# New instruction lengths and waiting rules in the planner that orders a macaron layer's instructions

## The chip, the cores and the metric

The kernel runs on one core of one Trainium2 chip. The metric is the device time of one execution in microseconds (us), taken as the median of several executions. The core has five instruction queues that matter here. PE is TensorE, the matrix engine; DVE is VectorE; ACT is ScalarE; POOL is GpSimd; SP is SyncE, which issues every DMA of this kernel. Each of them works through its own list of instructions strictly in order, and they wait for each other by semaphores.

## The reference, cut to what matters

The input x is 4 x 2048 x 256. The layer is a "macaron": half a feed-forward block, attention, and half a feed-forward block again, each on a normalised x.

```python
x = x + 0.5 * ffn(layernorm(x), w_gate, w_up, w_down)
x = x + attn(layernorm(x), Wq, Wk, Wv)        # causal, one head of 256
x = x + 0.5 * ffn(layernorm(x), w_gate, w_up, w_down)

def ffn(x, w_gate, w_up, w_down):             # hidden width 704
    h = silu(fp4_linear(x, w_gate)) * fp4_linear(x, w_up)
    return fp4_linear(h, w_down)

def fp4_linear(x, w):                         # both sides rounded to FP4 in blocks of 16
    return einsum('bsk,nk->bsn', fp4(x), fp4(w))
```

`fp4` takes the largest absolute value of each block of 16, divides by it over 6, rounds to the nearest of eight magnitudes and multiplies the scale back. It is done to the inputs of all three linear maps, so x and h pass through DVE several times before each product.

## The kernel before, in words

The 2048 rows of each of the 4 batches are cut into 8 pairs of 128-row tiles, so there are 32 pairs in all. One pair goes through: load, first layernorm (`ln_first`), FP4 of x (`x1`), gate and up products (`gu1`), FP4 of h (`hh1`), down product (`down1`), second layernorm (`lnattn`), the transposed copy of x for attention (`xattn`), the value and the key-side products (`vy`), scores, softmax (`exps`), weights times values (`pv`), third layernorm (`lnlast`), and the second feed-forward block (`x2`, `gu2`, `hh2`, `down2`). `step(n)` writes these stages for different pairs beside each other: pair n is in its scores while pair n+4 is in its gate and up products and n-2 in its second block. The last pair is cut into its two tiles, which go one behind the other.

Names that the text uses, with who writes them:

- `xn` normalised x (ACT), `xt` the running x in float32. A layernorm is: row sums, squares with row sums (ACT), a chain of seven small operations on POOL that ends in the mean times the inverse deviation (`fnm`, `anm` or `gnm` by stage), and the scaling back on ACT.
- `xs`, `xinv`, `xsh`, `xsl` block scales of x, `xf` its FP4 value; `xqT` the transposed halves of x that PE reads (a DMA transpose issued by SP).
- `pg`, `pu` PSUM results of gate and up, one buffer of two banks each; `h` is Silu of `pg` (ACT) times `pu` (DVE). Until Silu has read `pg`, the next gate product can't start.
- `hs`, `hinv`, `hsh`, `hsl`, `hf`: the same steps for h; `hT` its transposed halves. `po` (two buffers) takes the down product and is added to `xt` by DVE.
- `y` (`y16`) the key-side product, `vv` the values, `xT` transposed x, `ps` scores (two buffers), `sc` scores in SBUF, `pp` and `pT` softmax weights and their transposes.
- `gu`, `gwork`, `dwork`, `dw`, `wguT`, `wdT`, `tops`, `mx`, `cwp`: the preparation of the weights, FP4 as well, which runs once at the start beside the first pairs.

The order of the instructions isn't the order of the Python. Every operation is recorded (`Record`, `Op`) with what it reads and writes, and then `Record.order` plans: `_cost` gives each operation two lengths, `busy` (how long its engine is taken) and `late` (when its result can be seen), and each pair of dependent operations gets a lag. `_pass` then plays the program: at each point it takes the engine that can start first, and on it the waiting operation with the best rank, where being not ready yet costs `patience` and a change of the activation table costs `SWITCH`. A pass backwards gives new ranks, and six rounds of this for each of the fifteen entries in `POLICIES` are compared by `_lost`, PE's idle time in the first 500 us and after it in the planner's own clock. The best entry for each half is taken, and the list that results is what `emit` issues, one queue per engine (line 362, which is why every instruction of the profile is put down to that line). The planner's clock has no influence at run time: it only sets the order in each queue. What is computed, by which engine and in which buffers, is fixed.

In `_pass` three resources have rules of their own. DMA transposes are served one after the other (`served`). POOL shares its way to SBUF with some DVE operations (`op.locks`: two wide inputs, or a `tensor_scalar` on 16-bit data, none from PSUM): before the change a POOL operation is put off to the end of the DVE operation running (`locked`), and while one is put off (`kept`), DVE operations that lock are ranked lower by `PORT`. A change of activation table delays the operation by 1290.

Of the kernel before, what the change touches and what calls it, by code (L numbers as in the profile page):

```python
# [17 lines left out]
AF = mybir.ActivationFunctionType  # L18
ALU = mybir.AluOpType
# [33 lines left out]
LN2 = 0.6931471805599453  # L53
BYTES = {F32: 4, I32: 4, F16: 2, BF16: 2, U16: 2}
SWITCH = 17600.0
PORT = 500.0
ROUNDS = 6
POLICIES = [(soon, 60.0, lead) for lead in (0.0, 10000.0, 20000.0) for soon in (50.0, 100.0, 150.0, 200.0, 300.0)]
MIDDLE = 500000.0
# [1 line left out]
LATENCY = 1900.0  # L61
# [93 lines left out]
class Record:  # L155
# [53 lines left out]
    def _cost(self, op):  # L209

        size = lambda v: v.at.size
        views = op.outs + op.ins
        n = max(map(size, views[:1] + (op.ins[:1] if op.method == "tensor_reduce" else [])))
        psum = any(v.tile.pool.psum for v in views)
        accum = isinstance(op.kwargs.get("accum_out"), View)
        if op.engine == "PE":
            t = max(n, 64) / 2.4 + 2.2
            if op.ins[0].dtype == F32:
                t *= 2 if op.method == "transpose" or "is_transpose" in op.kwargs else 4
            return t, t + 65  # L220
        if op.engine == "SP":
            if op.method == "dma_start_transpose":
                return 1240, 2250 + max(0, n - 500) * 1.2
            op.load = n * 4 * P / RATE if op.outs else 0
            return 490, LATENCY + op.load + 500 * (not op.outs)
        if op.engine == "POOL":
            t = 110 if op.method == "memset" else 850 if ALU.pow in op.args else 350
            return t, t
        if op.engine == "ACT":
            t = 95 + n * (0.75 if psum else 0.833) + 90 * accum  # L230
            t += 90 * sum(isinstance(op.kwargs.get(k), View) for k in ("scale", "bias"))
            return t, t + 105 * (not accum)
        many = sum(size(v) > 1 for v in op.ins)
        op.locks = not psum and (many > 1 or op.method == "tensor_scalar" and BYTES[op.ins[0].dtype] == 2)
        fast = not psum and all(BYTES[v.dtype] == 2 for v in views)
        if op.method == "reciprocal":
            t = 60 + 6.25 * n
        else:
            t = 65 + n * (1.042 if not fast else 0.26 if op.method == "tensor_scalar" else 0.52) + 65 * accum
        return t, t + 95  # L240

    def order(self):

        for pool in self.pools:
            for ring in pool.rings.values():
                for k, t in enumerate(ring):
                    if k >= t.n:
                        t.first.deps.update(dict.fromkeys(ring[k - t.n].ops, True))  # L250
                    if k:
                        t.first.deps.setdefault(ring[k - 1].first, False)
                    t.first.deps.pop(t.first, None)
        for op in self.ops:
            for u in op.after:
                op.deps.setdefault(u, False)
            op.users = {}
        for op in self.ops:
            for u, data in op.deps.items():
                u.users[op] = u.late + 24 if data else u.busy  # L260

        best = [None, None]
        for policy in POLICIES:
            lead = {op: op.lead * policy[2] for op in self.ops}
            rank = {op: 88.0 * op.index - lead[op] for op in self.ops}
            for _ in range(ROUNDS):
                start, out, end = self._pass(rank, False, policy, policy)
                for h, value in enumerate(self._lost(start, end)):
                    if best[h] is None or value < best[h][0]:
                        best[h] = (value, policy, start, rank)  # L270

                back, _, _ = self._pass({op: -start[op] - op.busy for op in self.ops}, True, policy, policy)
                rank = {op: -back[op] - op.busy - lead[op] for op in self.ops}
        (_, one, start, rank1), (_, two, _, rank2) = best

        part = {op: min(1.0, max(0.0, (start[op] - MIDDLE) / 50000.0 + 0.5)) for op in self.ops}
        rank = {op: rank1[op] * (1.0 - part[op]) + rank2[op] * part[op] for op in self.ops}
        return self._pass(rank, False, one, two)[1]
# [7 lines left out]
    def _pass(self, rank, back, one, two):  # L286


        free = dict.fromkeys(("PE", "ACT", "DVE", "POOL", "SP"), 0.0)
        waiting, held = {e: [] for e in free}, ("PE", "POOL")  # L290
        ready, start = dict.fromkeys(self.ops, 0.0), {}
        if back:
            nxt, left = {op: [] for op in self.ops}, {op: len(op.users) for op in self.ops}
            for op in self.ops:
                for v, lag in op.users.items():
                    nxt[v].append((op, v.busy + lag - op.busy))
        else:
            nxt, left = {op: list(op.users.items()) for op in self.ops}, {op: len(op.deps) for op in self.ops}
        for op in self.ops:
            if not left[op]:  # L300
                waiting[op.engine].append(op)
        kept = False
        table, out, end, landed, served, locked, clock = None, [], 0.0, 0.0, 0.0, 0.0, Counter()
        while len(out) < len(self.ops):
            best = None
            if not any(waiting.values()):
                raise RuntimeError("the order goes in a circle")
            for e, ops in waiting.items():
                if ops:
                    t = max(free[e], min(ready[op] for op in ops))  # L310
                    if best is None or t < best[0]:
                        best = (t, e)
            t, e = best
            soon, patience = (one if t < MIDDLE else two)[:2]
            now = [op for op in waiting[e] if ready[op] <= t + soon]
            op = min(now, key=lambda o: (
                rank[o] + patience * max(0.0, ready[o] - t) + SWITCH * (o.table is not None and o.table != table)
                + PORT * (kept and e == "DVE" and o.locks)
            ))
            t = max(t, ready[op])  # L320
            if e == "POOL" and not back and op.method != "memset":

                kept = t < locked
                if kept:
                    free[e] = locked + 1.0
                    continue
            if op.table is not None and op.table != table:
                table, t = op.table, t + 1290
            waiting[e].remove(op)
            out.append(op)  # L330
            start[op], more = t, 0.0
            if back:
                pass
            elif e == "PE":

                k = int(t // WINDOW)
                more = op.busy if k and clock[k - 1] < IDLE * WINDOW else 0.0
                clock[k] += op.busy + more
            elif op.load:
                landed = max(landed, t + LATENCY) + op.load  # L340
                more = landed - t - op.late
            elif e == "SP" and op.outs:
                served = max(served + 1.7 * op.outs[0].at.size + 100, t + op.late)
                more = served - t - op.late
            elif e == "DVE" and op.locks:
                locked = t + op.busy
            elif e == "POOL" and op.method != "memset":
                more = (775.0 if ALU.pow in op.args else 275.0) - op.busy
            free[e] = t + op.busy + (more if e in held else 0.0)
            end = max(end, t + op.late + more)  # L350
            for u, lag in nxt[op]:

                ready[u] = max(ready[u], t + lag + (more if e in held or u.deps.get(op) else 0.0))
                left[u] -= 1
                if not left[u]:
                    waiting[u.engine].append(u)
        return start, out, end
# [787 lines left out]
```

## Time and profile before

| | |
|---|---|
| runs of the kernel | median 1195.94 us of 3 (1193.82 to 1197.42) |
| the profiled execution | 1194.8 us, span from first to last instruction 1193.1 us |
| busy in the span | PE 1156.1, DVE 1064.1, ACT 845.4, POOL 254.9 us |
| matmuls | 8665 |
| activation table loads | 84, 107.8 us in all |
| TensorE clock granted | 0.999 of full over the span |
| DMA transposes on SP's queue | 152 `pT`, 128 `hT`, 65 `xqT`, 64 `xT`, 2 `wguT` |

PE is the engine to look at: it is busy for 97% of the span. A matmul is pipelined; the length that the profile gives it (274 ns for 256 columns) runs until its last result, while the next one starts after 110 ns. So PE's idle time in a stretch, not its instructions' lengths, tells what is lost there. In the same way DVE's and ACT's operations overlap their neighbours by some 0.08 us when they don't wait for each other.

### The profile page before, as it was taken

How to read it: one execution, taken by the hardware profiler on the slowest of the kernel's cores; microseconds unless marked ns; L12 is line 12 of the kernel's file. 1: busy time of each engine (PE TensorE's matmuls, PEld its weight loads, DVE VectorE, ACT ScalarE, POOL GpSimd, SP SyncE). 2: the span in 40 equal slices, each digit the busy share in tenths (PEclk: the TensorE clock that was granted, in tenths of full speed). 3: DMA queues.
4: the chain of work that ended last, by engine and by line, in shares of the span. 5: the costliest groups of instructions: out<-in, count | busy, mean ns of one | idle time of the engine just before them, and what ended most of it. 6: DMA issues, size and time to landing. Idle time of an engine off the chain costs nothing.

```text
span 1193.1 us, 23867 instructions
## 1 busy us (share of the span) xinstructions
PE 1156.1 (97%) x8665; PEld 843.8 (71%) x8665; DVE 1064.1 (89%) x2677; ACT 845.4 (71%) x1694; POOL 254.9 (21%) x706
## 2 busy tenths in 40 slices
PE   3999999999999999999999999999999999999997
PEld 1676677777687777777777777777777777777775
DVE  8998999998879999998888999999887999978776
ACT  8788886676568777775776986776758776766552
POOL 4122331121032222212222230222212222010020
PEclk9999999999999999999999999999999999999999
DMA  7353646763665565655755465666556454665553
GB/s 236 55 100 71 109 88 110 140 129 71 107 131 103 105 116 120 113 93 111 134 102 81 95 114 104 131 131 120 92 104 113 88 93 87 114 117 96 102 111 85
DMA packets 452710, 128.92 MB, mean 108 GB/s; under 512 B 434672, under 2 KB 451824, under 8 KB 452592
## 3 DMA queue, kind: packets, MB, share of 16 engines
q1 hardware_dynamic: 452592, 127.39, 57.0%
q8 instruction: 68, 1.11, 0.4%
q14 instruction: 50, 0.41, 0.1%
HBM read 11.34 MB, written 8.39 MB: 17 GB/s over the span
## 4 chain that ended last, share of the span: by engine, by line
PE 68%; DVE 15%; ACT 12%; issue 2%; DMA 2%; POOL 1%; SPq 0%; DVEq 0%; ACTq 0%
PE po L362 30%; PE pg L362 14%; PE pu L362 14%; PE ps L362 10%; DVE h L362 5%; ACT xn L362 3%; ACT L362 2%; DVE hs L362 2%; ACT hf L362 2%; ACT h L362 1%; DVE xt L362 1%; DMA hT<-h 1%; ACT pp L362 1%; DVE xs L362 1%; DVE sc L362 1%
## 5 line engine op out<-in xcount | busy, mean ns | idle before, releaser
L362 PEld LDWEIGHTS <-xqT 128*128 128x128 f16 x3072 | 299.7, 98 | 161.1 <-issue 6.2
L362 PE MATMUL po<-wdT,hT 128*128 128x256 f16 x2176 | 262.6, 274 | 5.9 <-DMA hT<-h 5.6
L362 PE MATMUL pg<-wguT,xqT 128*128 128x384 f16 (+1 forms) x1536 | 258.9, 312 | 4.3 <-ACT h L362 2.3
L362 PE MATMUL pu<-wguT,xqT 128*128 128x384 f16 (+1 forms) x1536 | 253.3, 312 | 0.1
L362 PEld LDWEIGHTS <-hT 128*128 128x128 f16 x2176 | 213.2, 98 | 39.8 <-DMA hT<-h 7.6
L362 PE MATMUL ps<-xT,y 128*128 128x512 f16 (+2 forms) x960 | 200.9, 347 | 1.0 <-DVE mc L362 1.0
L362 PE MATMUL po<-vv,pT 128*128 128x257 f16 (+1 forms) x1632 | 194.4, 272 | 0.4
L362 PEld LDWEIGHTS <-pT 128*128 128x128 f16 x1632 | 157.9, 97 | 33.3 <-issue 2.3
L362 ACT ACTIVATE h<-pg,cgu 128x704 f32<-128x704 f32 x128 | 108.1, 845 | 93.9 <-PE pg L362 91.2
L362 DVE TENSOR_TENSOR h<-h,pu 128x704 f32<-128x704 f32 x128 | 113.2, 884 | 50.9 <-PE pu L362 33.4
L362 PEld LDWEIGHTS <-y 128*128 128x128 f16 x960 | 90.9, 98 | 69.6 <-ACT y L362 1.2
L362 ACT ACTIVATE hf<-h 128x1408 f16<-128x1408 bf16 (+1 forms) x65 | 88.1, 1355 | 65.1 <-DVE h L362 65.0
L362 ACT ACTIVATE sc<-sc,nb,ksc 128x128 f32<-128x128 f32 (+7 forms) x64 | 82.7, 1292 | 38.6 <-DVE nb L362 38.0
L362 ACT ACT_TABLE_LOAD x84 | 107.8, 1283 | 2.1 <-PEq L1138 0.8
L362 DVE TENSOR_REDUCE hs<-h 128x88 f32<-128x1408 f32 (+1 forms) x65 | 103.7, 1595 | 1.0
L362 DVE TENSOR_TENSOR h<-h,hinv 128x1408 f32<-128x1408 f32 (+1 forms) x65 | 103.8, 1597 | 0.4
L362 DVE TENSOR_SCALAR_CACHE_REDUCE sc<-ps 128x512 f32<-128x512 f32 (+2 forms) x144 | 84.7, 595 | 11.5 <-PE ps L362 11.2
L362 DVE TENSOR_TENSOR pp<-sc,pp 128x1024 f16<-128x1024 f32 (+4 forms) x96 | 86.1, 907 | 5.7 <-ACT pp L362 5.0
L362 POOL TENSOR_SCALAR gve<-gsq 128x2 f32<-128x2 f32 (+1 forms) x33 | 9.4, 284 | 380.3 <-ACT xn L362 380.2
L362 POOL TENSOR_SCALAR ave<-asq 128x2 f32<-128x2 f32 x32 | 14.1, 439 | 327.4 <-ACT xn L362 277.7
L362 ACT CAST pp<-sc 128x1024 f16<-128x1024 f32 (+4 forms) x96 | 73.1, 789 | 1.0
L362 DVE SCALAR_TENSOR_TENSOR xt<-po,het,xt 128x256 f32<-128x256 f32 x128 | 59.5, 464 | 11.7 <-PE po L362 11.6
(153 smaller groups left out, 1593.6 us busy)
## 6 DMA issues: line engine op xcount, KB each, us to landing
xt<-x SPq DMA_DIRECT2D x32, 256.0 KB, 3.3
out<-xt SPq DMA_DIRECT2D x31, 256.0 KB, 2.6
pT<-pp SPq DMA_TRANSPOSE x152, 3.0
hT<-h SPq DMA_TRANSPOSE x128, 3.8
gu<-wgu SPq DMA_DIRECT2D x3, 384.0 KB, 5.0
xqT<-xn SPq DMA_TRANSPOSE x65, 3.2
xT<-xs SPq DMA_TRANSPOSE x64, 2.5
dwork<-wdn SPq DMA_DIRECT2D x1, 704.0 KB, 7.3
```

The source lines that it names most:

```text
L362: op.call(*map(real, op.args), **{k: real(v) for k, v in op.kwargs.items()})
```

## The change

The diff touches `_cost`, the lags in `order`, and `_pass`; no operation, tile or buffer is changed. The numbers are nanoseconds in the planner's clock.

- Results of PE are seen 176 after the matmul's turn instead of 65. An ACT row sum is seen 105 later, where before it was seen at once; a DVE row sum costs 10 instead of 65. A DVE `tensor_scalar` or `scalar_tensor_tensor` with a per-row operand costs 62 more. Silu costs 33 more.
- The lag from one engine to the next, 24 for all before, comes from `_lag`: 94 or 101 to POOL, 81 from PE to a DVE `tensor_tensor`, 48 from ACT to PE, 24 otherwise.
- POOL operations cost 154, 647 for the power, and are seen 28 later. They are no longer put off before they are chosen: each waits, once chosen, for the one locking DVE operation that was running then. `PORT` is gone, and POOL takes only operations that are ready.
- SP's transposes cost it 1280 and more, and are queued: `served` counts 1400 and 1.26 per element, the result is seen 450 later, and SP itself is held to within 1850 of the queue's end. Other DMA issues cost 570 instead of 490.
- A change of table lets the operation start 1400 after the one before it on ACT has ended, instead of 1290 after it was ready.

```diff
-PORT = 500.0
@@ _cost
-            return t, t + 65
+            return t, t + 176
         if op.engine == "SP":
             if op.method == "dma_start_transpose":
-                return 1240, 2250 + max(0, n - 500) * 1.2
+                return 1280 + 0.13 * n + 0.75 * max(0, n - 1408), 1850 + 1.26 * n
             op.load = n * 4 * P / RATE if op.outs else 0
-            return 490, LATENCY + op.load + 500 * (not op.outs)
+            return 570, LATENCY + op.load + 500 * (not op.outs)
         if op.engine == "POOL":
-            t = 110 if op.method == "memset" else 850 if ALU.pow in op.args else 350
-            return t, t
+            t = 110 if op.method == "memset" else 647 if ALU.pow in op.args else 154
+            return t, t + 28
...
-            return t, t + 105 * (not accum)
+            t += 33 * (AF.Silu in op.args)
+            return t, t + 105
...
-            t = 65 + n * (1.042 if not fast else 0.26 if op.method == "tensor_scalar" else 0.52) + 65 * accum
+            t = 65 + n * (1.042 if not fast else 0.26 if op.method == "tensor_scalar" else 0.52) + 10 * accum
+            t += 62 * (op.method in ("tensor_scalar", "scalar_tensor_tensor") and any(size(v) == 1 for v in op.ins[1:]))
         return t, t + 95
+    def _lag(self, u, op):
+        if op.engine == "POOL":
+            return 94 if u.engine == "POOL" else 101
+        return 81 if u.engine == "PE" and op.method == "tensor_tensor" else 48 if u.engine == "ACT" and op.engine == "PE" else 24
@@ order
-                u.users[op] = u.late + 24 if data else u.busy
+                u.users[op] = u.late + self._lag(u, op) if data else u.busy
@@ _pass
+            if e == "POOL":
+                soon = 0.0
...
-                + PORT * (kept and e == "DVE" and o.locks)
...
-            if e == "POOL" and not back and op.method != "memset":
-                kept = t < locked
-                if kept:
-                    free[e] = locked + 1.0
-                    continue
             if op.table is not None and op.table != table:
-                table, t = op.table, t + 1290
+                table, t = op.table, max(t, free[e] + 1400)
...
             elif e == "SP" and op.outs:
-                served = max(served + 1.7 * op.outs[0].at.size + 100, t + op.late)
-                more = served - t - op.late
+                served = max(served, t + 1400) + 1.26 * op.outs[0].at.size
+                more = served + 450 - t - op.late
+                free[e] = max(t + op.busy, served - 1850)
             elif e == "DVE" and op.locks:
-                locked = t + op.busy
+                locked = [locked[1], (t, t + op.busy)]
             elif e == "POOL" and op.method != "memset":
-                more = (775.0 if ALU.pow in op.args else 275.0) - op.busy
-            free[e] = t + op.busy + (more if e in held else 0.0)
+                more = max([0.0] + [hi - t - 35.0 for lo, hi in locked if lo <= t < hi])
+            free[e] = max(free[e], t + op.busy + (more if e in held else 0.0))
```

More of the change, by code (lines that the diff above doesn't have):

```diff
@@ L301, in _pass @@
                 waiting[op.engine].append(op)
-        kept = False
-        table, out, end, landed, served, locked, clock = None, [], 0.0, 0.0, 0.0, 0.0, Counter()
+        table, out, end, landed, served, locked, clock = None, [], 0.0, 0.0, 0.0, [(0.0, 0.0)] * 2, Counter()
         while len(out) < len(self.ops):
```

## The prediction

> **What bounds the kernel now.** I read the busy times first, then the idle time of PE by stage, then what ended it in the stages where there is any, and last the order of the instructions.
>
> ```profile
> PE 1156.1 (97%) x8665; PEld 843.8 (71%) x8665; DVE 1064.1 (89%) x2677; ACT 845.4 (71%) x1694; POOL 254.9 (21%) x706
> ```
>
> PE is idle for 1193.1 - 1156.1 = 37.0 us. The next view gives busy times by stage (the number after the colon is the stage's length, then PE, weight loads, DVE, ACT, POOL, and the granted clock).
>
> ```profile
> 0.00:20.00 20.00, 1.20 (x4) 0.82 (x5) 14.63 (x41) 14.84 (x47) 6.60 (x30) 1.00 0.93 309
> 20.00:60.00 40.00, 36.59 (x238) 24.88 (x238) 39.28 (x92) 31.01 (x74) 9.90 (x24) 1.00 0.35 64
> 60.00:200.00 140.00, 135.46 (x1020) 98.06 (x1019) 131.03 (x342) 113.24 (x244) 39.04 (x110) 1.00 0.56 99
> 200.00:1150.00 950.00, 948.41 (x7153) 694.63 (x7151) 848.87 (x2122) 671.15 (x1299) 194.97 (x529) 1.00 0.58 107
> 1150.00:1194.00 44.00, 34.43 (x259) 25.40 (x256) 30.29 (x84) 15.14 (x33) 4.37 (x14) 0.96 0.47 101
> ```
>
> The idle time is 18.8, 3.4, 4.5, 1.6 and (up to 1193.1) 8.7 us. Four fifths of the span hold 1.6 of it. DVE is at 98% from 20 to 60 us: there the weights are prepared on DVE beside the first pairs, and DVE is the bound. The timeline shows the places:
>
> ```profile
> 5.25 0.45 DVE L362 RECIPROCAL dwork<-gwork 128x48 f32<-128x48 f32 x1
> 6.71 0.95 DVE L362 TENSOR_REDUCE gwork<-gu 128x48 f32<-128x768 f32 x1 [1.01 <-DMA gu<-wgu]
> 19.75 1.54 PE L362 MATMUL pg<-ident,gu 128*128 128x128 f32 x6 [3.12 <-DVE gu L362]
> 21.65 1.80 DVE L362 TENSOR_REDUCE dwork<-dwork 128x88 f32<-128x1408 f32 x1
> 31.79 0.97 PE L362 MATMUL pg<-wguT,xqT 128*128 128x384 f16 x5 [0.66 <-ACT h L362]
> 98.40 0.81 PE L362 MATMUL ps<-xT,y 128*128 128x512 f16 x3 [0.96 <-DVE mc L362]
> 1156.47 1.95 PE L362 MATMUL pg<-wguT,xqT 128*128 128x384 f16 x12
> 1158.46 1.28 ACT L362 ACT_TABLE_LOAD   x1
> 1159.75 0.85 ACT L362 ACTIVATE h<-pg,cgu 128x704 f32<-128x704 f32 x1
> 1179.40 7.41 PE L362 MATMUL po<-wdT,hT 128*128 128x256 f16 x51 [3.77 <-DMA hT<-h]
> 1187.67 2.03 PE L362 MATMUL po<-wdT,hT 128*128 128x256 f16 x17 [0.86 <-DMA hT<-h]
> ```
>
> **The change part by part.** It removes no instruction. Counted in the queues: 8660 matmuls, 84 table loads, 411 transposes and 73 other DMAs, before and after. Its whole effect is the order, so I price the four stretches where PE idles. A DVE step is the time from its start to the next one's, about its length less 0.08.
>
> *Head, to 60 us.* Three moves on DVE, before the first transposes of `gu`. The reciprocal, which ran in the wait for the second load, goes behind the 6.71 reduction: +0.45. The 1.80 reduction of `dwork` comes ahead of `cwp`: +1.7. The rounding of the last `gu` part goes behind: -0.2. With some waits for ACT (+0.3) the transposes start at 22.0 instead of 19.75. Before the second set stand the scales and two products of another part (0.23 + 2 x 0.47): 24.05 instead of 21.1. PE's queue now also has the `dwork` maximum (`mx`) and `tops`, DVE's 52nd step, ahead of the first real product: about 27.1 instead of 24.3. Most of this is taken back, since all that DVE did early is no longer due. `dw`, next on DVE, ends at 31.1 against 30.3; the table load stands behind both `df` and the next row sums and starts at 30.75 against 29.59, so Silu frees `pg` at 32.95 and PE goes on there instead of at 31.79. Followed on, PE starts the second pair's products about 1.0 us behind what it had done before, and is still about 1.2 behind at 51 us. SP's first transposes move with DVE and end ahead of PE's need but for tenths. I take +1.0. Ends: 0, if DVE's 98% alone sets this stage, as its total work is the same; +2.8, if nothing is taken back.
>
> *Ramp, 60 to 200 us* (4.5 idle). The clearest loss is at 98.40: PE's queue had the scores directly behind the 12 matmuls that make `y`, which still needs 0.59 on ACT and 0.68 on DVE. Now five value matmuls and three gate matmuls stand between, 5 x 0.11 + 3 x 0.16 = 1.0 us. I take -0.9. The waits for `xT` (1.2) and `hT` (1.0) I leave: the shortest PE work between the last `pu` of a pair and the first use of its `hT` is 12.2 us here before and 13.6 after, and the row's own steps add up to about as much. Ends: -4.5, all idle gone; +4.5, as much again.
>
> *Middle, 200 to 1150 us* (1.6 idle). The work in PE's queue between a producer and its reader is long on both sides: median 29.3 before and 28.2 after from `pu` to `hT`, 32.0 and 31.0 from scores to `pT`. This covers later PE results, POOL's chains and queued transposes. The tight place is Silu: where `pg` is asked for again after less than 1.6 us of PE work the whole queue had 3 cases of 128 and now has 6. Three more at the 0.2 us that was the longest such wait in this stage is +0.5. Ends: -1.6; and, from the ramp's rate, far away, 950 x 4.5 / 140 = +31. I stay by the stage's own row, since the work between producer and reader is its own, not the ramp's.
>
> *Tail, from 1150 us.* Call the end of the last `pv` matmuls T (1156.5 before). Ten gate matmuls of the pair before the last move ahead of T: T is 1.5 us later, and as much less work stands behind it. The table load also comes before T, so Silu ends at T+1.25 instead of T+4.1, while the second tile's layernorm comes behind it: its scaling at T+5.6 instead of T+5. By the DVE steps in the new order PE then waits 0.75 for the second `xqT`, 3.8 for `hT` (3.77 before), 0.7 and 1.25 for the last two `hT`. The last one leaves DVE at T+25.1, lands 3.5 later, and PE ends at T+30.6, against 1189.7 = T+33.2 before. With T 1.5 later: -1.1. DVE no longer stands 0.65 for a `po` ahead of its last `hf` step; that is in it. I take -1.0. Ends: -3.0 (both short waits also gone) and +2.0 (the order's DVE work ahead of those last products is 0.9 longer than before between the same PE marks, and T itself may come late).
>
> After the wait of 3.77 us the 51 matmuls took 7.41 us instead of 51 x 0.11 = 5.6, at a granted clock of 0.88 in the last 14 us. The Trainium skill, page "TensorE: Matmul & The Clock Gate", Part 1, says that one idle window of about 3.4 us halves the clock for the next; by it a wait just below that would save 1.8 us of matmuls. I count no such saving, since the last `hT` lands after them in either case.
>
> The table loads: the row has 84 at 1283 ns, and the next ACT operation starts 1.29 us after the load does, so 1400 for a switch is ample. The page "ScalarE: Activation LUTs", section "What ACT_TABLE_LOAD costs", adds a drain of some 1.38 us to each switch; this trace doesn't show it. By the page Silu in the tail would end about 0.1 later, and the sum would be -0.3 instead of -0.4.
>
> Sum: +1.0 - 0.9 + 0.5 - 1.0 = -0.4 us on the profiled execution of 1194.8, that is 1194.4. The median of the runs is 1.1 above that execution, so **1195.5 us**. A difference of 0.3% (3.6 us) is about what a measurement of this kernel can tell from no change.
>
> **The rivals.** (a) *The better lengths pay everywhere.* All idle of the ramp and 3 us of the tail go: -7.5, 1188.4. For it: at 98.40 and in the tail the order does avoid waits that the old lengths hid (a matmul of 256 columns lasts 274 ns, not its turn plus 65). Against: to 60 us DVE is the bound, and its work is the same. (b) *GpSimd's chain becomes the bound (slower).* With the penalty gone, DVE may put locking operations back to back while POOL's chain waits. A POOL operation of 191 ns has taken up to 1581; the seven of a chain could take 9 us more. Behind it ACT stands at `xn`, and in 20 places of the new ACT queue (17 before) Silu is next, whose delay reaches PE once it exceeds about 0.75 us, which 12 `pu` matmuls (1.79) leave beside Silu. If ten of them then cost 0.7, the longest wait of PE for Silu in the whole trace, it is +7.0: 1202.9. For it: ACT already waits 30.2 us for POOL. Against: only 2.3 us of PE's waits are for Silu. (c) *The change does nothing*: another order of the same quality, 1195.9; for it, 1.6 us of idle in the middle leave nothing to mend.
>
> **How the numbers follow.** Forecast 0.47, (c) 0.10, (a) 0.20, (b) 0.23. Forecast and (c) lie within 0.3%, so the chances are faster 0.20, same 0.57, slower 0.23. The range runs from near (a), 1189.5, to (b), 1203.0: what lies beyond it is the far part of (a), and a middle worse than (b), some 2 in 10. The forecast's own range, without the far ends of ramp and middle, is 1192.5 to 1198.5.
>
> **What would show it.** PE's idle time by stage: about 23 to 60 us, 3.6 in the ramp, 2 in the middle, 7.5 in the tail. First `pg<-ident,gu` near 22, first product with `xqT` near 27, no wait of a microsecond between `y` and the scores, the table load before the last `pv` ends, and a wait of about 3.8 for `hT`. POOL's summed time tells of (b): it should stay near 255, and PE's waits for Silu near 2.8. I am wrong if the middle idles by more than 5 us, or if the head doesn't start its products later.

## The result and the profile after

The changed kernel takes 1198.57 us (median of 17 runs, 1197.71 to 1201.11), the kernel before 1195.94 us beside it (17 runs). The ratio is 1.0026, with a 95% interval of 1.0019 to 1.0033: slower by a quarter of a percent. The profiled execution took 1197.7 us and has a span of 1195.9 us, against 1194.8 and 1193.1 before: +2.9 and +2.8.

First the page's busy times, the DMA queue that will matter, and the same stages as before (busy us of PE, weight loads, DVE, ACT, POOL, then the granted clock).

```profile
PE 1157.1 (97%) x8665; PEld 846.1 (71%) x8665; DVE 1058.6 (89%) x2677; ACT 844.9 (71%) x1694; POOL 248.1 (21%) x706
...
q8 instruction: 68, 1.11, 0.4%
```
```profile
0.00:20.00 20.00, 0.96 (x3) 0.58 (x3) 14.65 (x38) 14.77 (x48) 9.04 (x34) 1.00 0.97 312
20.00:60.00 40.00, 37.19 (x231) 25.23 (x231) 38.37 (x92) 31.22 (x72) 8.28 (x22) 1.00 0.31 59
60.00:200.00 140.00, 133.55 (x1002) 97.39 (x1001) 127.76 (x337) 113.90 (x242) 35.64 (x105) 0.99 0.55 95
200.00:1150.00 950.00, 946.97 (x7150) 694.27 (x7148) 843.89 (x2126) 670.09 (x1302) 190.38 (x533) 1.00 0.60 108
1150.00:1196.00 46.00, 38.48 (x285) 28.60 (x283) 33.93 (x88) 14.88 (x33) 4.72 (x14) 0.91 0.51 105
```

PE's idle time to 60 us is 21.9 (22.2 before), in the ramp 6.5 (4.5), in the middle 3.0 (1.6), and from 1150 us to the end of the span 7.4 (8.7 in a tail that began with more work left). The granted clock is 0.99 in the ramp and 0.91 in the tail, where it was 1.00 and 0.96. What PE waited for from 60 to 1150 us (engine, output, releaser: us, times, longest), after:

```profile
PE po L369 <- DMA hT<-h: 5.9, 4, 2.1
PE po L369 <- DMA pT<-pp: 1.7, 1, 1.7
PE ps L369 <- DVE sc L369: 1.4, 2, 0.9
PE pg L369 <- DMA xqT<-xn: 0.2, 1, 0.2
PE po L369 <- DMA xT<-xs: 0.2, 1, 0.2
```

Before, the same view has 1.2 for Silu, 1.0 for `mc`, and for transposes:

```profile
PE po L362 <- DMA xT<-xs: 1.2, 2, 0.7
PE po L362 <- DMA hT<-h: 1.0, 2, 0.8
```

PE's waits for transposes cost 8.0 us now and cost 2.2 before. The timeline of PE shows where, and what the predicted steps became (start, length, idle before in brackets):

```profile
21.21 1.54 PE L369 MATMUL pg<-ident,gu 128*128 128x128 f32 x6 [4.62 <-DVE gu L369]
...
27.11 2.30 PE L369 MATMUL pg<-wguT,xqT 128*128 128x384 f16 x6 [0.44 <-ACT wguT L369]
...
61.24 3.65 PE L369 MATMUL po<-wdT,hT 128*128 128x256 f16 x29 [0.89 <-DMA hT<-h]
...
77.34 5.55 PE L369 MATMUL po<-wdT,hT 128*128 128x256 f16 x34 [2.13 <-DMA hT<-h]
...
114.27 2.03 PE L369 MATMUL po<-wdT,hT 128*128 128x256 f16 x17 [1.48 <-DMA hT<-h]
...
132.27 0.83 PE L369 MATMUL po<-wdT,hT 128*128 128x256 f16 x6 [1.38 <-DMA hT<-h]
...
438.33 1.94 PE L369 MATMUL po<-vv,pT 128*128 128x257 f16 x16 [1.66 <-DMA pT<-pp]
...
1174.84 1.96 PE L369 MATMUL pg<-wguT,xqT 128*128 128x384 f16 x12 [0.53 <-DMA xqT<-xn]
...
1182.10 10.41 PE L369 MATMUL po<-wdT,hT 128*128 128x256 f16 x68 [3.51 <-DMA hT<-h]
```

Four waits, 2.13 + 1.48 + 1.38 + 1.66 = 6.65 us, stand out. In each the transpose, three of `hT` and one of `pT`, took 5.31 to 5.33 us from issue to landing. In the 58 cases in the two traces where an `hT` transpose was issued with no other transpose in flight and no packet of code came during its transfer (from 1 us behind the issue to the landing), it took 3.51 to 3.90 us; 32 of `pT`, of all widths, took 2.29 to 4.85. So I looked at what else the DMA engines did. Here are two stretches of the DMA view of the kernel after: one that begins at the late transpose of 71.97 us (landed 77.30), and one at a transpose of the same size at 229.44 us (landed 233.13). The first two rows of each are the busy tenths of the 16 DMA engines and GB/s in 40 slices; the line on q8 counts packets, MB and share.

```profile
DMA  0000000006999999999999999996000100002999
GB/s 0 0 0 0 0 0 0 0 2 140 222 216 218 212 210 190 218 216 201 160 169 196 226 223 343 194 108 7 0 0 4 9 7 11 9 9 39 287 290 289
...
q8 instruction: 1, 0.02, 1.0%
...
hT<-h SPq DMA_TRANSPOSE x2, 5.1
```
```profile
DMA  9910000004999999999999999999999999999999
GB/s 289 205 13 0 0 0 0 0 0 95 217 225 217 208 216 205 217 214 192 171 201 200 245 225 214 214 205 207 225 212 207 129 147 175 250 257 226 210 214 216
...
hT<-h SPq DMA_TRANSPOSE x2, 3.9
```

In the first, the transfer runs for some 2.5 us, then there is a tail of a microsecond in which at most one or two of the 16 engines are busy and move 4 to 11 GB/s, and the next transpose's packets come only behind it. In the second, without a packet on q8, the next transpose follows at once. Queue q8 carries 68 packets of 16 KB in the whole run, one per 127 matmuls. I take it to bring PE's own instructions; the experiments bear that out, since extra matmuls in front move the packets. A packet takes about a microsecond (0.88 to 1.65, median 0.96), on one of the 16 engines. In all four waits such a packet started 2.1 to 3.5 us behind the transpose's issue. Of the `hT` transposes issued with no other in flight, 7 in before (median 5.09 us) and 12 in after (median 5.31 us) met one, and it matters when: the 7 whose packet started at most 1.3 us behind the issue took 3.80 to 4.66 us, the 11 whose packet started 3.1 to 3.8 us behind took 5.09 to 5.85. Nine more met only an 8 KB packet of another instruction queue, q14, and took 3.71 to 4.24.

The Trainium skill, page "DMA: Bandwidth & Descriptors", section "Queues, rings and completion order", says that each DMA engine takes turns between the queues it has work for, a whole packet at a time, and that one DMA is spread over up to 16 engines. That fits the tail on one engine. The page "Trainium Architecture — The Big Picture", section "The software stack", says that instruction streams are moved to the engines when the program is loaded. That sentence doesn't cover what the trace shows: 68 packets came during the run, and the measurement decides.

To see where the time goes I compare the two traces at equal work: the moment at which PE has the same number of matmul columns behind it (extra matmuls not counted). The numbers are us behind the kernel before, at before's 53.8, 192 and 1136 us and at the last matmul; the lower rows belong to experiments told below.

| kernel | 53.8 us | 192 us | 1136 us | last matmul |
|---|---|---|---|---|
| after | +1.3 | +3.4 | +3.1 | +2.8 |
| after, 128 extra matmuls | +3.0 | +3.5 | +2.8 | +3.5 |
| after, 48 extra matmuls (short) | +3.7 | -0.4 | -1.1 | -2.2 |
| after, 88 extra matmuls (short) | +1.0 | -2.5 | -4.5 | -4.2 |

The loss of the kernel after arises before 192 us, and from there on nothing is lost.

### The profile page after: what moved, and what is told of

Same layout as the page of the kernel before. It is cut to its first block, busy times and chain, and to the rows that moved or that the text cites. A ratio compares the mean times of both kernels' runs of the same rounds, so it can differ in the third digit from the quotient of the medians.

```text
span 1195.9 us, 23892 instructions
## 1 busy us (share of the span) xinstructions
PE 1157.1 (97%) x8665; PEld 846.1 (71%) x8665; DVE 1058.6 (89%) x2677; ACT 844.9 (71%) x1694; POOL 248.1 (21%) x706
## 4 chain that ended last, share of the span: by engine, by line
PE 86%; DVE 5%; DMA 3%; ACT 3%; POOL 1%; issue 1%; SPq 0%; ACTq 0%; DVEq 0%
PE po L369 38%; PE pg L369 17%; PE pu L369 17%; PE ps L369 13%; DMA hT<-h 2%; DVE h L369 2%; ACT xn L369 1%; DVE hs L369 1%; DMA xqT<-xn 0%; DMA gu<-wgu 0%; DMA pT<-pp 0%; DVE xn L369 0%; DVE xt L369 0%; ACT sc L369 0%; DVE sc L369 0%
```

## The experiments

Theory F: the four waits come from transposes that meet one of PE's code packets, not from the order as such. Theory O: the new order puts the readers too close behind their transposes whatever the packets do. Later rivals are named where they come up. All ratios are to runs of the kernel before on the same chip.

**Moving the packets, leaving the order.** In the trace a packet comes once per 127 matmuls. Extra matmuls at the front of PE's queue, where PE has nothing to do, should shift all packets to earlier places in an order that stays the same. They write to a PSUM tile that the first real operation overwrites.

```diff
+FILL = 48
...
     def emit(self, ops):
...
+        first = next(op for op in ops if op.engine == "PE")
+        filler = next(op.outs[0] for op in ops if op.engine == "ACT")
         for op in ops:
+            for _ in range(FILL if op is first else 0):
+                op.call.__self__.matmul(
+                    View(op.outs[0].tile, op.outs[0].at, P, F32, ()).real()[:, :P], real(filler), real(filler),
+                    start=True, stop=True,
+                )
```

The kernel after with 48 of them:

> The changed kernel with 48 extra matmuls (and weight loads) at the very front of PE's queue, where PE otherwise idles; the order of everything else is that of the change. Theory F (instruction fetch): the trace after shows that PE's code comes in packets of 16 KB on a DMA queue of its own, one for each 128 matmuls, and that a transpose in flight at that moment lands about 1.7 us late; four such meetings make PE wait 2.13 us at 77, 1.48 at 114, 1.38 at 132 and 1.66 at 438 us, and 1.5 us more of matmuls at half clock behind the first. With 48 matmuls more, each packet is asked for 48 matmuls (about 6.5 us) earlier in the order, and by the traced times no transpose with less than 1.7 us to spare meets one: the four waits fall to about 0.4 together, time 1191 to 1193.5. Rival O (the new order asks for the transposes too early by its own lengths, whatever the packets do): same waits at the same places, 1198.5.

Measured: 1192.77 us, ratio 0.9973 (0.9963 to 0.9984). The packet that came at 75.2 us comes at 69.4, and the waits at 114, 132 and 438 us are gone; PE's waits for `hT` from 60 to 200 us:

```profile
PE po L377 <- DMA hT<-h: 1.5, 3, 0.8
```

A new meeting at 53 us costs 1.34, one at 1122 us 0.97. With 12 of them, as a control:

> The changed kernel with 12 extra matmuls at the front. A control for the longer one: the extra work is there, but the packets move by 1.6 us only, and by the traced times they still meet the hT transposes before 114 and 132 us and, less surely, that before 77 us. Theory F: 1196.5 to 1199. Rival O: 1198.5. If the extra matmuls help in themselves (a warm clock at the head), this one gains as the one with 48 does.

Measured: 1196.02 us, ratio 0.9998 (0.9989 to 1.0007), a little below what I expected. The waits at 77 us (2.08) and 437 us (1.25) are still there, that at 114 us is down to 0.70, that at 132 us is gone, and a new one of 1.00 stands at 690 us. The same in the kernel before:

> The kernel before with the same 48 extra matmuls at the front. Theory F: its packets are moved onto transposes with little to spare (xT near 65, hT near 99, pT near 749 us); PE's idle time in them goes from 3.5 to about 6.0 us, time 1197.5 to 1199.5. Rival O, or extra matmuls that help in themselves: 1196 or less.

> The kernel before with 12 extra matmuls at the front. Theory F: the one meeting that cost it something (hT before 129.7 us, 0.8 us) goes away, nothing comes in its place: 1194 to 1195.5. Rival O: 1196.

Measured: 1196.77 us, ratio 1.0001 (0.9992 to 1.0010), and 1196.21 us, ratio 1.0005 (0.9997 to 1.0014). Neither went as I had worked it out. With 48 the predicted meeting of `xT` is there (1.74 us at 70.8), the others cost little. With 12 the wait at 129.7 us went away as expected, but the packets met others: 0.95 at 89 us, 1.07 at 688, and 2.22 in place of 0.86 at the last `hT`. The direction for the kernel after is clear; a sum over single meetings isn't to be had this way.

What remained possible was that the extra matmuls act by what they do in the head (rival H): in the profiles with 48 long ones the clock was granted by halves for 13.7 us there. Shorter ones of 16 columns, and as many as one whole packet, tell that apart, since 128 extra matmuls should put all but the first packets back to where they were:

```diff
-                    View(op.outs[0].tile, op.outs[0].at, P, F32, ()).real()[:, :P], real(filler), real(filler),
+                    View(op.outs[0].tile, op.outs[0].at, P, F32, ()).real()[:, :16], real(filler), real(filler)[:, :16],
```

> The changed kernel with 48 extra matmuls of 16 columns at the front of PE's queue (the earlier 48 had 128 columns and held PE longer; four half-clock windows stood in the head). Theory F: 1191.5 to 1193.5, no wait for hT at 77, 114 and 132 us. Rival H (the extra matmuls act by what they do in the head): shorter ones act less, 1194 to 1198.

> The same with 88 extra matmuls of 16 columns. Theory F: by the traced times of after, packets asked for 88 matmuls earlier (or 40 later) meet transposes with little to spare in other places (xqT asked for near 61, xT near 98, pT near 153 and 341 us): 6.3 us of waits in sum against 6.7 without extra matmuls and 1.7 with 48; 1195.5 to 1198.5. Rival H: 1190 to 1193.5, as more of them help as much or more.

> The same with 128 extra matmuls of 16 columns: a whole packet more, so every other packet is asked for where it was in the kernel after. Theory F: the waits of 2.1, 1.5, 1.4 and 1.7 us near 77, 114, 132 and 438 us come back; 1197 to 1199.5, slower than before again. Rival H: 1190 to 1193.5.

> The kernel before with the same 128 extra matmuls. Theory F: its packets stay where they were, 1195.5 to 1197. Rival H: 1190 to 1194.

Measured: 48 short ones 1192.62 us, ratio 0.9974 (0.9964 to 0.9983); 88 give 1191.09 us, 0.9961 (0.9946 to 0.9976); 128 give 1198.70 us, 1.0026 (1.0016 to 1.0035); the kernel before with 128 gives 1195.78 us, 0.9996 (0.9987 to 1.0005). With a whole packet more the changed kernel has its old time back, and its waits in the old places:

```profile
79.14 3.88 PE L377 MATMUL po<-wdT,hT 128*128 128x256 f16 x34 [2.06 <-DMA hT<-h]
...
114.37 2.03 PE L377 MATMUL po<-wdT,hT 128*128 128x256 f16 x17 [1.45 <-DMA hT<-h]
...
132.38 0.83 PE L377 MATMUL po<-wdT,hT 128*128 128x256 f16 x6 [1.37 <-DMA hT<-h]
```

The wait for `pT` is back as well, at 437.7 us, with 0.87 of its 1.66. One and the same order takes from 1191.1 to 1198.7 us, and the waits go and come with the packets, so for the four waits theory O and rival H fall. That the two ratios of 1.0026 are equal to the last digit is partly luck: with 128 extra matmuls the head is 1.7 us later, and the clock isn't halved behind the wait at 79 us (34 matmuls in 3.88 us, not 5.55).

My reckoning of single places failed again at 88: of the meetings near 61, 98, 153 and 341 us that I had worked out none cost PE anything, and the one that did, 1.48 for a `pT` at 1149.6 us, I hadn't. Its wait for `xT` at 83 us (0.52) has no packet in it; for the `xqT` of the wait at 100 us (0.76) a packet ended just as the transfer began. The packets don't keep so exact a place: in the trace after, 8 of 10 start between the 60th and the 85th matmul of their 128, which is a spread of 3.4 us at 0.134 us per matmul. With 88 the ramp stands so:

```profile
60.00:200.00 140.00, 137.24 (x1042) 100.42 (x1043) 131.97 (x347) 117.31 (x251) 36.68 (x108) 1.00 0.57 101
```

Idle in the ramp is 2.8 us, against 6.5 without extra matmuls and 4.5 in the kernel before.

**Leaving room for the packets.** If meetings are what costs, a planner that expects transposes to land later has other work ready. Either every transpose lands 1.65 us later, or only those that meet the packet of each 128th matmul:

```diff
-                return 1280 + 0.13 * n + 0.75 * max(0, n - 1408), 1850 + 1.26 * n
+                return 1280 + 0.13 * n + 0.75 * max(0, n - 1408), 3500 + 1.26 * n
...
-                more = served + 450 - t - op.late
+                more = served + 2100 - t - op.late
```
```diff
                 clock[k] += op.busy + more
+                done += 1 + (op.method == "matmul" and op.ins[0].dtype == F32)
...
                 more = served + 450 - t - op.late
+                code = free["PE"] + (85 - done) % 128 * 134.0
+                if t + 1000 < code < served + 450:
+                    more += 1650
```

> The changed planner with every transpose taken to land 1.65 us later than the change has it, whether it meets a packet or not. Theory F: no wait for a met transpose is left but those under 0.3 us; in the ramp, where little other work is at hand, chains grow longer, so the gain is smaller than that of the planner that knows the packets: 1192 to 1196. Rival O: 1198 or more, since longer chains only delay the ramp.

> The changed planner, told of PE's code packets as well: it counts matmuls, expects a packet at every 128th (85, 213, ...), and adds 1.65 us to the landing of a transpose whose transfer meets it. Theory F: the order may again bring packets and transposes together, but PE's queue then has other work between them and the reader; PE's waits for transposes that met a packet fall from 6.65 us to under 2, and the clock isn't halved behind one; 1191 to 1194. Rival O (the lengths of the change are themselves too short in the ramp): the first waits stay, 1196 to 1199. Rival N (any new order is another draw, and the knowledge of the packets is drowned by their jitter of a microsecond): 1193 to 1199, with packets met in new places.

Measured: with the margin 1192.28 us, ratio 0.9974 (0.9962 to 0.9986); with the packets counted 1192.70 us, 0.9973 (0.9964 to 0.9981). Both gain what moving the packets gained. With the margin PE has no wait for a transpose at all from 60 to 1150 us; its longest there is 1.8 for `y`. It pays at the end, where a wait of 5.59 us for `hT` replaces 3.51. The counted packets leave three meetings of 1.10, 0.94 and 0.60 us. The same two edits in the planner before ask whether the new lengths are worth anything (theory L) or whether the room does it all (theory M):

```diff
-                return 1240, 2250 + max(0, n - 500) * 1.2
+                return 1240, 3900 + max(0, n - 500) * 1.2
```
```diff
                 more = served - t - op.late
+                code = free["PE"] + (85 - done) % 128 * 134.0
+                if t + 1000 < code < served:
+                    more += 1650
```

> The planner before, lengths untouched, but every transpose taken to land 1.65 us later. It tells whether the new lengths of the change are worth anything once the met transposes are covered. Theory L (the new lengths gain, and the packets hid it): the waits for met transposes go (about 1.5 us in before), but those at other lengths stay: 1194 to 1196.5, 2 us or more behind the changed planner with the same margin (1192.3). Theory M (the margin does it all, the new lengths are worth nothing): 1191 to 1193.

> The planner before, lengths untouched, but told of PE's code packets as the changed one was (1.65 us more for a transpose whose transfer meets the packet of each 128th matmul). Theory L: 1194 to 1196.5. Theory M: 1191 to 1193.5. If it comes out above 1197, another draw of the order counts for more than either.

Measured: 1195.21 us, ratio 0.9987 (0.9978 to 0.9995), and 1198.13 us, 1.0010 (1.0001 to 1.0018). With the same room the new lengths are ahead by the ratios, 0.9974 against 0.9987 (1.6 us) and 0.9973 against 1.0010 (4.4 us). That speaks for theory L, but weakly: in the first pair the intervals overlap, and two pairs of orders are few. With the packets counted the order before met packets all the same (at 75 and 111 us, and at the last `hT`, 2.57), so part of the 4.4 may be another draw.

Two more kernels have a wider test for a meeting, and half of each remedy on top of that test:

```diff
-                if t + 1000 < code < served + 450:
+                if t + 400 < code < served + 1050:
```
```diff
-                return 1280 + 0.13 * n + 0.75 * max(0, n - 1408), 1850 + 1.26 * n
+                return 1280 + 0.13 * n + 0.75 * max(0, n - 1408), 2650 + 1.26 * n
...
-                more = served + 450 - t - op.late
+                more = served + 1250 - t - op.late
...
-                    more += 1650
+                    more += 850
```

> The changed planner with the packets as before, but a meeting is expected from 0.4 us behind the issue to 0.6 us behind the landing, since three met transposes still cost 1.1, 0.9 and 0.6 us with the narrow window: their packets came a little beside the time that the count gives. Theory F: those waits go, PE idles 2 us less from 60 to 1150 us; 1190 to 1192.5, if the end of the order doesn't come out worse (it idled 8.4 us in the last 35 us of the narrow one, so 1193.5 if it does again). Rival N (each order is another draw of plus or minus 3 us): anywhere from 1190 to 1198.

> The changed planner with 0.8 us more for every transpose and 0.85 more for one that is expected to meet a packet. Theory F: no wait of more than 0.5 us for a met transpose, 1190 to 1192.5. Rival N: 1190 to 1198.

Measured: 1196.57 us, ratio 0.9997 (0.9988 to 1.0006), and 1192.30 us, 0.9960 (0.9948 to 0.9972). The wide test missed: three meetings are back, with packets 2.8 to 4.0 us behind the issue.

```profile
79.80 1.38 PE L374 MATMUL po<-wdT,hT 128*128 128x256 f16 x11 [1.67 <-DMA hT<-h]
...
116.15 2.03 PE L374 MATMUL po<-wdT,hT 128*128 128x256 f16 x17 [1.53 <-DMA hT<-h]
...
133.10 0.61 PE L374 MATMUL po<-wdT,hT 128*128 128x256 f16 x4 [1.17 <-DMA hT<-h]
```

The place that I gave both planners, the 85th matmul of each 128, was read from the first dozen packets; over the whole run the median is the 72nd, 1.7 us earlier. Whether that is why, or whether the planner knew the meetings and had nothing else to give to PE, I didn't find out; nor do these runs exclude that each planner's order is simply another draw. Room for every transpose helped under both sets of lengths (0.9974, 0.9987); knowing the places alone helped in one of three (0.9973, against 0.9997 and 1.0010). The kernel with half of each still has a met `pT` that costs 0.85. It and the one with 88 extra matmuls have the lowest ratios of all, clear of the kernel before and the kernel after, but not of the 0.9974 with the margin.

**Early and late part exchanged.** Two fixed orders: what one planner starts ahead of 150 us by its own clock, then the rest in the other's order.

```diff
-        best = [None, None]
...
-        return self._pass(rank, False, one, two)[1]
+        import base64, zlib
+        return [self.ops[k] for k in np.frombuffer(zlib.decompress(base64.b85decode(ORDER)), np.uint16)]
```

> A fixed order: all that the planner before starts ahead of 150 us by its own clock, in the order before, then the rest in the order after. At equal matmul counts the traced kernel after stands 4.3 us behind before at matmul 900 (151.6 us), 2.8 at matmul 3000 and at the end. If the loss is all in the early part, as the traces have it, this one is 1.5 us faster than before, 1194 to 1195.5, its wait of 1.66 us near 434 us still there. If the late part of the order carries a loss of its own that the early lag hid: 1196.5 or more.

> The other way round: the order after for all that its planner starts ahead of 150 us, then the rest in the order before. By the same counts 4.3 us slower than before: 1199.5 to 1201, with the waits of 2.1, 1.5 and 1.4 us for hT at 77, 114 and 132 us. If the early lag is made up whatever follows it: 1197 to 1198.5.

Measured: 1198.76 us, ratio 1.0023 (1.0014 to 1.0032), and 1203.29 us, 1.0061 (1.0048 to 1.0074). The seam spoils the first: there PE waits for a Silu that stands behind a table load (157.02 us) on ACT, with a half-clocked stretch behind it.

```profile
159.21 3.07 PE L658 MATMUL pg<-wguT,xqT 128*128 128x384 f16 x12 [2.33 <-ACT h L658]
```

In it PE is even with before up to that place and 3.2 us behind past it. The second has a wait of 2.30 us at its seam. It had the early lag of 4.1 us (equal matmul counts) before the seam, with the `hT` waits of 2.1, 1.3 and 1.2 us, and nothing of it is made up later. So the pair confirms that the early part holds a loss that stays, and leaves open what the late part alone is worth.

## Why the prediction was wrong

I forecast -0.4 us on the profiled execution; it was +2.9. The range held the time, and the 0.26% lie within the 0.3% that I gave 0.57, but the direction was wrong. By steps, as gains or losses at equal work:

- *Head, +1.0:* +1.3. The first `pg<-ident,gu` came at 21.2 (I said 22.0), the first product with `xqT` at 27.1 (27.1), and most of the delay was taken back, as I had followed it. This step was right.
- *Ramp, -0.9:* +2.1. **This is the step that failed**, and in it the sentence "The waits for `xT` (1.2) and `hT` (1.0) I leave". The wait between `y` and the scores did go, as predicted. But I gave the `hT` transposes one duration, the row's, where the trace of before already held both 3.6 and 5.2 us, and called 13.6 us of PE work behind `pu` as safe as 12.2. The order after puts the readers about where an unmet transpose lands; three that met a packet then cost 4.99 us, where before paid 0.80 for one. The first of them also left PE idle for so long that the clock was halved: 34 matmuls took 5.55 us, where the same 34 take 3.88 in the kernel with 128 extra ones; there, with the waits but not the halved clock, the ramp's step is +0.5. A fourth wait for `hT`, 0.89 at 61.2 us, met no packet and stays when the packets move (0.87 with 48 short extra matmuls, 0.86 with 88): that one is the order's own. With the packets elsewhere (88 extra) the ramp's step is -3.5, from +1.0 to -2.5. So the new order can gain more in the ramp than the 0.9 that I priced, and the packets outweighed it; how much of that is the better lengths and how much the draw isn't shown.
- *Middle, +0.5:* idle rose by 1.4, but at equal work the stage gave -0.3. None of the waits for Silu that I priced came; the rise holds one met `pT`, 1.66 us.
- *Tail, -1.0:* -0.3. The waits came as worked out (0.53 for 0.75, 3.51 for 3.8), and the two short ones at the end fell away. But the last 68 matmuls took 10.41 us, against 7.41 + 2.03 before: 6.8 us of half clock instead of 3.4. I had counted nothing for the clock.
- *Rival (b), GpSimd:* its summed time fell from 254.9 to 248.1 us, and no wait of PE for Silu is left from 60 to 1150 us. It wasn't this. Its working had a misread row, too: 1581 ns was the power operation's, which takes 690 at least; an operation of 191 ns took up to 1651 in the trace of before. *Rival (a)*, better lengths pay everywhere, 1188.4: with 88 extra matmuls the order takes 1191.1, still 2.7 above it.

What I had right is the course of the head and the waits of the tail; what I lacked is that a landing time has a wide spread, and where in it a transpose lands is set by something that the order moves without meaning to.

## What to carry to other kernels

Before pricing a new order, read the spread of each DMA's landing time, not its median, and ask of every long one what shared its engines; instruction packets are on the page as a queue of their own. Two orders that differ by half a percent may differ only in where PE's code packets fall, so test an order with some extra matmuls in front before judging it. In these runs it was the safer course to plan for each transpose to land 1.65 us later (a gain in both tries) than to reckon where the packets come (a gain in one of three).

## What was not expected of the hardware

- A 16 KB packet of PE's code, about 1 us on one DMA engine, once per 127 matmuls, delays an `hT` transpose in flight: 3.51 to 3.90 us without, 3.80 to 5.85 with one, the more the later it starts in the transfer. `xqT` and `xT` show it too: `xqT` takes 3.05 (median) without, and of three in before whose packet started 2.3 to 2.7 us behind the issue two took 4.7 and one 3.07; `xT` takes 2.41 without, and the one of the 1.74 us wait in before with 48 extra matmuls took 4.30.
- Moving the packets alone changed one order's time by 7.6 us of 1198.7, and 128 extra matmuls, a whole packet, brought the waits and the time back (ratio 1.0026, as without).
- The clock. The Trainium skill, "TensorE: Matmul & The Clock Gate", Part 1, speaks of an idle window of about 3.4 us. Here a wait of 2.13 us was enough when it fell into one window, and one of 2.06 us did nothing when it straddled two. The windows (us, PE busy, weight loads, DVE, ACT, POOL, clock) after, and with 128 extra matmuls:

```profile
75.15:78.57 3.42, 1.29 (x13) 1.11 (x13) 3.42 (x4) 1.22 (x3) 0.00 (x0) 1.00 1.24 166
78.57:81.99 3.42, 3.42 (x19) 2.42 (x17) 1.53 (x8) 0.65 (x2) 0.00 (x0) 0.50 0.42 85
```
```profile
77.31:80.73 3.42, 1.59 (x15) 1.43 (x16) 3.42 (x6) 0.92 (x2) 0.00 (x0) 1.00 1.03 151
80.73:84.14 3.41, 3.41 (x34) 2.90 (x32) 2.30 (x10) 1.16 (x4) 0.00 (x0) 1.00 0.38 77
```

PE was busy for 38% of the window ahead of the halved one, and for 46% of the window that was followed by the full clock. So a window needn't be idle as a whole. From 60 us on, two windows of other runs narrow it down: one with PE busy for 39% (75.41 us, after with 12 extra matmuls) was followed by half clock, one with 42% (1175.28 us, before with 12) by the full clock. Before 60 us it doesn't hold: in the kernel with half of each remedy a window with 47% (30.79 us) was followed by half clock. Why stays open.
